# Three 16-head attentions in one kernel: the two halves of each step's scores in a row, the outputs of two steps together, other work behind every second step

## The chip, the core and the metric

The kernel runs on one core of a Trainium2 chip. Its time is the device time of a run in microseconds (us). The core's engines work side by side, each on its own queue in its own order: TensorE (PE, with its weight loads shown apart as PEld), VectorE (DVE), ScalarE (ACT), GpSimd (POOL) and SyncE (SP), which here issues transfers. Semaphores between them hold an instruction until what it reads, or the buffer that it writes, is ready.

## What is computed

The reference is a decoder of two layers on `x` of 4 x 512 tokens, 256 wide. Each layer adds an attention, a cross attention with a context of 1024 tokens, and a feed-forward part to `x`. The change touches three of these, all with 16 heads of 16: the cross attention of the first layer, and the causal attention and the masked cross attention of the second.

```
x = x + L0_attn(layernorm(x));  x = x + L0_xattn(layernorm(x), ctx);  x = x + L0_ffn(layernorm(x))
x = x + L1_attn(layernorm(x));  x = x + L1_xattn(layernorm(x), ctx, mask);  x = x + L1_ffn(layernorm(x))

# L1_xattn; L0_xattn is the same without a mask, L1_attn is causal over the 512 tokens and has a rotation of q and k
query, key_, value = q @ w_q.T + b_q, k @ w_k.T + b_k, v @ w_v.T + b_v         # as [b, 16 heads, s, 16]
scores = einsum('bhqd,bhkd->bhqk', query, key_) / sqrt(16)
scores = where(mask == 0, -1e9, scores)
out = einsum('bhqk,bhkd->bhqd', softmax(scores), value)
return out @ w_o.T + b_o
```

## The kernel before

`heads16` runs these attentions: once for the first layer's cross attention (four parts, one per batch), once for the second layer's two (four causal parts, then four masked ones). A part has four groups `g` of four heads. Each head has 32 partitions of its own, so that four score products can stand on four groups of 32 rows of TensorE at once (`tile_position`). A step is a group and one block of 128 keys: a cross attention has eight steps per group, a causal one four.

The softmax is shifted by each query's largest score, and these maxima are taken ahead of use. So `step(t, u, heads)` does two things at once. For step `t` it makes the transposed scores of four heads (`pa`, L586), whose exponentials ACT writes into `pT` (L605; three buffers). For a step `u` further on it makes plain scores (`pb`, L593), of which DVE takes the row maxima (L626, or L629 where a mask is added). Every product takes a tile of `k.ps()`, a ring of seven PSUM banks (`pools16`); the eighth bank, `av`, gathers outputs. `heads` says which heads of `t` are done; `pb` is shifted by two, so that half a step, two `pa` and two `pb`, fills the four row groups. Products in 32-bit floats are carried out as two passes, and the profile counts each pass.

Where a mask stands, heads 2 and 3 get it by a product of `mask_kT` and a unit matrix on TensorE (L600), heads 0 and 1 by a minimum with `keep_kT` on DVE (L615). In a causal step POOL zeroes the triangle (L609), and the widths shrink: 512, 384, 256 and 128 columns for the four key blocks.

`output` (L661) multiplies `pT` with the values, on four column groups, and adds into `av`; after a group's last block ACT copies `av` to `un` (L669). `lowest` (L638, L641) gathers the maxima of a group, `fold` (L646, L651) transposes them and adds them to the queries three and two steps ahead of the group's first step. `divide` (L676 to L682), `turn` (L693, L698) and `rows` finish a group, a pair and a part. The preparation of the parts to come (norms, projections of queries, keys and values on L125, transfers by `spread`), the making of the masks, and the beginning of what follows are cut into units that `lay` spreads over the slots.

The order is written out by hand for PE, DVE, POOL and SP (`manual_schedule`); ACT's is left to the scheduler. A loop goes over `slots`, each with a step `t`, a step `u`, or both. In every slot with both it issues the first half of the step (heads 0 and 1), then the output of an earlier step (`late` steps back, one in the first run, two in the second), then the second half, then the units in `todo` for this slot.

Of the kernel before, what the change touches and what calls it, by code (L numbers as in the profile page):

```python
# [34 lines left out]
def t_(pool, shape, dtype, tag, bufs=None):  # L35
    return pool.tile(list(shape), dtype, name=tag, tag=tag, bufs=bufs)
# [479 lines left out]
def heads16(k, work, parts, more=(), tail=()):  # L516
# [4 lines left out]

    nc = k.nc
    ng = 4 * len(parts)
    part = lambda g: parts[min(g, ng - 1) // 4]
# [2 lines left out]
    late = 1 if plain else 2  # L529
    start = [0]  # L530
# [3 lines left out]
    total = len(seq)  # L534

    slots, pos, ptr = [], {}, 0
# [10 lines left out]
    def slot(t):  # L547
        return pos[0] + t if t < 0 else pos[t] if t < total else pos[total - 1] + t - total + 1
# [3 lines left out]
    def on_pe(g, h):  # L552
        return part(g).masked is not None and h >= 2

    def step(t, u, heads):


        pa, pb = {}, {}
        if t:
            g, kb = t  # L560
            this = part(g)
            kT, c = batch[g // 4][1], g % 4
            q0 = kb * P if this.causal else 0
            w = S - q0
            if t not in pts:
                pts[t] = t_(work, [P, 4, 512], F32, "pT", 3)
            pT = pts[t]
        if u:
            ug, s = u
            other = part(ug)  # L570
            nh = other.nk // 512
            uqT, ukT = batch[ug // 4][:2]
            uc = ug % 4
            qb, kh = ((1, 0, 3, 2)[s], 0) if other.causal else divmod(s, nh)
            uw = (qb + 1) * P if other.causal else 512
            if ug not in mx:
                mx[ug] = t_(work, [P, TB, nh, 4], F32, f"mx{nh}", 3)
        for h in heads:
            if t:
                pa[h] = k.ps()  # L580
            if u:
                pb[(h + 2) % 4] = k.ps()
        for h in heads:
            if t:
                rows = slice(h * 32, h * 32 + 32)
                nc.tensor.matmul(  # L586
                    pa[h][:, :w], lhsT=kT[rows, c, kb * P : (kb + 1) * P], rhs=q2s[g][rows, q0:],
                    start=True, stop=not on_pe(g, h), tile_position=(h * 32, 0),
                )
            if u:  # L590
                r = (h + 2) % 4
                rows = slice(r * 32, r * 32 + 32)
                nc.tensor.matmul(  # L593
                    pb[r][:, :uw], lhsT=uqT[rows, uc, qb * P : (qb + 1) * P],
                    rhs=ukT[rows, uc, kh * 512 : kh * 512 + uw],
                    start=True, stop=True, tile_position=(r * 32, 0),
                )
        for h in pa:
            if on_pe(g, h):
                nc.tensor.matmul(  # L600
                    pa[h], lhsT=k.identb, rhs=this.masked["mask_kT"][:, kb, :], start=False,
                    stop=True,
                )
        for h in pa:
            nc.scalar.activation(pT[:, h, :w], pa[h][:, :w], AF.Exp)  # L605
        if t and this.causal:

            block = pT[:, heads[0] : heads[-1] + 1, 0:P]
            nc.gpsimd.affine_select(  # L609
                out=block, in_=block, compare_op=ALU.is_ge, fill=0.0, base=0,  # L610
                pattern=[[0, len(heads)], [1, P]], channel_multiplier=-1,
            )
        if t and this.masked and heads[-1] == 3:

            nc.vector.tensor_tensor(  # L615
                pT[:, 0:2], pT[:, 0:2],
                this.masked["keep_kT"][:, kb, :].unsqueeze(1).to_broadcast([P, 2, 512]), ALU.min,
            )
        for r in pb:
            to = mx[ug][:, qb, kh, r : r + 1]  # L620
            if other.causal:
                mask = k.ahead[:, 512 - uw :]
            elif other.masked:
                mask = other.masked["mask_q"][:, qb, kh * 512 : kh * 512 + 512]
            else:
                nc.vector.tensor_reduce(to, pb[r], AX.X, ALU.max)  # L626
                continue
            junk = t_(work, [P, 512], BF16, "junk", 1)
            nc.vector.tensor_tensor_reduce(  # L629
                out=junk[:, :uw], in0=pb[r][:, :uw], in1=mask,  # L630
                scale=1.0, scalar=-3.0e38, op0=ALU.add, op1=ALU.max, accum_out=to,
            )
# [20 lines left out]
    def output(g, kb):  # L653
        v, c = batch[g // 4][2], g % 4
        nkb = size(g)
        q0 = kb * P if part(g).causal else 0
        pT = pts.pop((g, kb))
        if kb == 0:
            avs[g] = t_(k.avp, [P, 512], F32, "av")
        for h in range(4):  # L660
            nc.tensor.matmul(  # L661
                avs[g][h * 32 : h * 32 + 32, q0:],
                lhsT=v[:, kb, (c * 4 + h) * 32 : (c * 4 + h) * 32 + 32],
                rhs=pT[:, h, : S - q0], start=kb == 0, stop=kb == nkb - 1,
                tile_position=(0, h * 32),
            )
        if kb == nkb - 1:
            uns[g] = t_(work, [P, 512], F32, "un", 1)
            nc.scalar.copy(uns[g], avs.pop(g))  # L669
# [30 lines left out]
    def rows(j, i):  # L700
        parts[j].y_rows(i, oTs[j][:, :, i * P : (i + 1) * P])

    todo, load_ = {}, {}

    def at(i, f, *x, pe=0.0):
        todo.setdefault(i, []).append((f, x))
        load_[i] = load_.get(i, 0.0) + pe

    def lay(lo, hi, calls):


        if hi <= 0:
            for f, _ in calls:
                f()
            return
        lo = max(lo, 0)
        there = [load_.get(i, 0.0) + 0.01 for i in range(lo, hi)]
        whole = sum(there) + sum(c for _, c in calls)
        i, sofar = 0, there[0]
        for f, c in calls:  # L720
            while i < hi - lo - 1 and sofar + c / 2 > whole * (i + 1) / (hi - lo):
                i += 1
                sofar += there[i]
            at(lo + i, f, pe=c)
            sofar += c

    marks = []
    for j in range(len(parts)):
        g = start[4 * j]
# [9 lines left out]
    def begin(j):  # L739
        qT, kT, v, chains = parts[j].prep(marks[j])  # L740
        batch[j] = qT, kT, v
        return chains

    ET = mybir.EngineType
    with k.tc.manual_schedule(engines={ET.PE, ET.DVE, ET.Pool, ET.SP}):
        for g in range(ng):
            end = slot(start[g + 1] + late)
            at(slot(start[g] - 3), lowest, g)
            at(slot(start[g] - 2), fold, g, pe=0.45)
            at(end, divide, g, pe=0.45)  # L750
            if g % 2:
                at(end + 1, turn, g, pe=0.45)
            if g % 4 == 3:
                for i in range(TB):
                    at(end + 2 + i // (1 if size(g) > 4 else 2), rows, g // 4, i, pe=0.9)
        for j in range(len(parts)):
            for chain in begin(j):
                lay(*chain)
        for lo, hi, calls in tail:
            lay(len(slots) + lo, len(slots) + hi, calls)  # L760
        for i, u in enumerate(more):
            at(pos[0] + 2 + i * (total - 4 * size(0) - 4) // len(more), u)
        for i in range(len(slots) + late + 6):
            t, u = slots[i] if i < len(slots) else (None, None)
            this = seq[t] if t is not None else None
            ahead = seq[u] if u is not None else None
            both = this and ahead
            if this or ahead:
                step(this, ahead, (0, 1) if both else (0, 1, 2, 3))
            done = t - late if t is not None else i - len(slots) + total - late  # L770
            if (t is not None or i >= len(slots)) and 0 <= done < total:
                output(*seq[done])
            if both:
                step(this, ahead, (2, 3))
            for f, x in todo.pop(i, ()):
                f(*x)


def pools16(k, ctx, name):
# [63 lines left out]
def l0_xattn(k, a):  # L843
    with ExitStack() as ctx:
        wp, work = pools16(k, ctx, "l0x")
        bufs, preset = padded(k, wp, SC)
        k.masked, more = masks(k, work, a)
        parts = cross(k, a, "l0x_", wp, work, bufs, preset)
        heads16(k, work, parts, more=more, tail=ffn_begun(k, a, work))
# [1252 lines left out]
```

## Time and profile before

| what | value |
|---|---|
| median of three runs | 3626.74 us (3625.46 to 3632.22) |
| the profiled execution: time, span | 3623.15 us, 3621.4 us |
| mean granted TensorE clock | 0.966 |
| busy: PE, DVE, ACT, POOL | 94%, 59%, 42%, 27% |
| first cross attention, about | 1031 to 1530 us |
| causal attention, about | 1965 to 2243 us |
| masked cross attention, about | 2243 to 2893 us |

The span is the time from the first to the last instruction of one profiled execution; the run's own time has a little around it. A row of the groups gives line, engine, operation, tiles and count, then the busy time and the mean of one in ns, then the engine's idle time just before them and what ended it. A row of the timeline gives start, length, engine and instruction, with neighbours of one form merged (x2), and in brackets the idle time before it and what released it. PE's instructions overlap, so that the distance from start to start is the time that counts.

### The profile page before, as it was taken

The page shows a single profiled execution, that of the slowest core. Times are in us where ns is not written, and L with a number is a line of the kernel's source. Part 1 is how long each engine was busy: PE and PEld are TensorE (multiplying, and loading weights), DVE is VectorE, ACT ScalarE, POOL GpSimd, SP SyncE. Part 2 cuts the span into 40 slices and gives each one's busy share as a digit, 9 for nine tenths or more (in the row PEclk, how much of TensorE's full clock was granted, in tenths as well). Part 3 has the DMA queues.
Part 4 walks back from the last instruction along what each step waited for, and adds up shares of the span by engine and source line. Part 5 has one row for each costly group of instructions (what it writes and reads, how often), then busy time and mean ns, then how long its engine had stood idle before and what let it go on. Part 6 is the DMA issues. An engine that isn't in the chain of part 4 may idle for free. (4 is left out here: it accounts for less than half of the span.)

```text
span 3621.4 us, 51832 instructions
## 1 busy us (share of the span) xinstructions
PE 3419.2 (94%) x19168; PEld 1593.0 (44%) x19168; DVE 2142.3 (59%) x4804; ACT 1538.0 (42%) x3346; POOL 965.8 (27%) x1185
## 2 busy tenths in 40 slices
PE   7899999997799999999997999999999999999999
PEld 3445454453443333345554444333333344444444
DVE  3575666755477666747785677888888722222211
ACT  2546555465445555554442444445445511111111
POOL 2342433423311021326673322000000022222222
PEclk8899999998899999999997999999999999999999
DMA  3423223241121101000002111010010042111111
GB/s 124 163 82 130 101 96 111 69 152 59 40 41 39 39 27 40 7 21 15 1 1 47 47 44 42 18 24 13 18 28 1 1 156 84 53 47 53 50 52 44
DMA packets 119885, 197.51 MB, mean 55 GB/s; under 512 B 12624, under 2 KB 62800, under 8 KB 117456
## 3 DMA queue, kind: packets, MB, share of 16 engines
q1 hardware_dynamic: 118368, 189.68, 17.2%
q10 hardware_dynamic: 1264, 4.52, 0.4%
q8 instruction: 151, 2.47, 0.3%
q14 instruction: 102, 0.84, 0.1%
HBM read 129.67 MB, written 51.90 MB: 50 GB/s over the span
## 5 line engine op out<-in xcount | busy, mean ns | idle before, releaser
L605 ACT ACTIVATE pT<-ps 128x512 f32<-128x512 f32 (+3 forms) x1280 | 650.9, 565 | 626.4 <-PE ps L593 343.7
L593 PE MATMUL ps<-kT,qT 32*128 32x512 f32 (+3 forms) x2560 | 798.1, 618 | 23.6 <-DMA kT<-way 8.9
L586 PE MATMUL ps<-q,kT 32*128 32x512 f32 (+3 forms) x2560 | 690.6, 609 | 6.8 <-DVE mx L626 6.1
L125 PE MATMUL big<-xnT,w 128*128 128x512 f32 x1024 | 460.3, 592 | 0.0
L1702 DVE TENSOR_TENSOR gu<-big,silu 128x512 f32<-128x512 f32 x136 | 94.1, 692 | 563.5 <-ACT silu L1700 563.5
L626 DVE TENSOR_REDUCE mx<-ps 128x1 f32<-128x512 f32 x512 | 326.5, 685 | 164.2 <-PE ps L593 163.5
L629 DVE CUSTOM_DVE_ANT_0 junk<-ps,mask_q 128x512 bf16<-128x512 f32 x512 | 353.1, 690 | 95.2 <-PE ps L593 27.9
L586 PEld LDWEIGHTS ps<-q,kT 32*128 32x128 f32 x2560 | 214.5, 184 | 349.0 <-ACT pT L605 117.6
L1700 ACT ACTIVATE silu<-big 128x512 f32<-128x512 f32 x136 | 81.2, 597 | 603.8 <-PE big L125 603.8
L1706 POOL TENSOR_TENSOR gu<-gu,cb 128x512 f32<-128x512 f32 x128 | 163.5, 1277 | 633.8 <-DVE gu L1702 503.5
L661 PE MATMUL av<-pT,v 128*32 128x512 f32 (+3 forms) x2560 | 325.3, 578 | 0.5 <-ACT un L669 0.4
L252 POOL TENSOR_TENSOR st<-st,kerm 128x8 f32<-128x8 f32 (+51 forms) x256 | 190.5, 745 | 460.7 <-PE hp L248 398.2
L251 ACT ACTIVATE hd<-hd 128x16 f32<-128x16 f32 (+51 forms) x256 | 162.7, 636 | 344.5 <-DVE hd L250 344.4
L593 PEld LDWEIGHTS ps<-kT,qT 32*128 32x128 f32 x2560 | 259.7, 187 | 103.9 <-DVE mx L629 40.4
L125 PEld LDWEIGHTS big<-xnT,w 128*128 128x128 f32 x1024 | 194.6, 190 | 244.9 <-issue 244.9
L1714 PE MATMUL acc<-gu,w 128*128 128x512 f32 x512 | 241.0, 593 | 1.1 <-POOL gu L1706 1.1
L248 PE MATMUL hp<-st,l0a_w1s 64*128 64x104 f32 (+26 forms) x1024 | 193.4, 456 | 48.6 <-DVE hd L250 48.3
L250 DVE TENSOR_TENSOR hd<-hp,hk 128x16 f32<-128x16 f32 (+51 forms) x256 | 178.5, 697 | 90.8 <-PE hp L248 85.3
L53 POOL TENSOR_TENSOR ln_rstd<-ln_rstd,mhalf 128x4 f32<-128x4 f32 x24 | 24.6, 1023 | 741.6 <-DVE ln_rstd L52 697.1
L260 PE MATMUL ps<-hd,l0a_w 128*64 128x104 f32 (+26 forms) x1024 | 171.4, 414 | 32.3 <-ACT hd L251 26.5
L629 DVE CUSTOM_DVE_ANT_0 junk<-ps,ahead 128x256 bf16<-128x256 f32 (+3 forms) x256 | 125.5, 490 | 75.6 <-PE ps L593 49.2
L1490 ACT ACTIVATE pr<-ps,nmax 128x512 f32<-128x512 f32 x128 | 87.1, 687 | 174.2 <-DVE nmax L1489 173.9
(303 smaller groups left out, 5053.8 us busy)
## 6 DMA issues: line engine op xcount, KB each, us to landing
cb<-comb SPq DMA_DIRECT2D x128, 256.0 KB
scr<-sc SPq DMA_DIRECT2D x108, 256.0 KB
st<-scr SPq DMA_DIRECT2D x16, 1024.0 KB
scr<-sc SPq DMA_DIRECT2D x64, 192.0 KB
st<-scr SPq DMA_DIRECT2D x16, 768.0 KB
w<-in_l1f_w SPq DMA_DIRECT2D x32, 384.0 KB
wqk<-in_l0a_wqk SPq DMA_DIRECT2D x32, 256.0 KB
st<-scr SPq DMA_DIRECT2D x16, 512.0 KB
```

The lines of the kernel that those rows point to most:

```text
L125: k.nc.tensor.matmul(out, lhsT=lhsT(c), rhs=rhs(c), start=start and c == 0, stop=stop and c == 1)
L248: nc.tensor.matmul(hp[:, half, :n], lhsT=w1s[rows], rhs=s[rows, :n], start=True, stop=True)
L250: nc.vector.tensor_tensor(hd[:, :, :n], hp[:, :, :n], hk[:, :, S - n :], ALU.add)
L252: nc.gpsimd.tensor_tensor(s[:, :n], s[:, :n], kerm[:, S - n :], ALU.add)
L260: nc.tensor.matmul(rp[half * 64 : half * 64 + 64, :n], lhsT=w2, rhs=hd[:, half, :n], start=True, stop=True,)
L586: nc.tensor.matmul(pa[h][:, :w], lhsT=kT[rows, c, kb * P : (kb + 1) * P], rhs=q2s[g][rows, q0:], start=True, stop=not on_pe(g, h), tile_po ...
L593: nc.tensor.matmul(pb[r][:, :uw], lhsT=uqT[rows, uc, qb * P : (qb + 1) * P], rhs=ukT[rows, uc, kh * 512 : kh * 512 + uw], start=True, stop ...
L605: nc.scalar.activation(pT[:, h, :w], pa[h][:, :w], AF.Exp)
L626: nc.vector.tensor_reduce(to, pb[r], AX.X, ALU.max)
L629: nc.vector.tensor_tensor_reduce(out=junk[:, :uw], in0=pb[r][:, :uw], in1=mask, scale=1.0, scalar=-3.0e38, op0=ALU.add, op1=ALU.max, accum ...
L661: nc.tensor.matmul(avs[g][h * 32 : h * 32 + 32, q0:], lhsT=v[:, kb, (c * 4 + h) * 32 : (c * 4 + h) * 32 + 32], rhs=pT[:, h, : S - q0], sta ...
L1714: nc.tensor.matmul(accs[b][:, n, :], lhsT=w[e][:, 512 + n * P : 512 + (n + 1) * P], rhs=g, start=e == experts[0], stop=e == experts[-1],)
```

## The change

Only the order in which `heads16` issues its work is changed.

- In every slot with both `t` and `u`, the two halves of the step are issued in a row.
- Outputs come behind every step with an even `t`: those of all steps up to `t - 1` that have not been made, which are two in the steady state. Behind odd steps there are none. After the last slot the rest follow.
- `lowest` and `fold` go into a list of their own, `now`, whose entries run in their slot, behind the outputs. They no longer count in the load that `lay` evens out.
- The other units of a slot (`todo`) run behind odd steps only, those of the even step before and of the odd one together, and behind slots without a `t`.

```diff
-    todo, load_ = {}, {}
+    now, todo, load_ = {}, {}, {}
...
-            at(slot(start[g] - 3), lowest, g)
-            at(slot(start[g] - 2), fold, g, pe=0.45)
+            now.setdefault(slot(start[g] - 3), []).append((lowest, g))
+            now.setdefault(slot(start[g] - 2), []).append((fold, g))
...
+        done = 0
         for i in range(len(slots) + late + 6):
             t, u = slots[i] if i < len(slots) else (None, None)
             this = seq[t] if t is not None else None
             ahead = seq[u] if u is not None else None
-            both = this and ahead
             if this or ahead:
-                step(this, ahead, (0, 1) if both else (0, 1, 2, 3))
-            done = t - late if t is not None else i - len(slots) + total - late
-            if (t is not None or i >= len(slots)) and 0 <= done < total:
+                if this and ahead:
+                    step(this, ahead, (0, 1))
+                    step(this, ahead, (2, 3))
+                else:
+                    step(this, ahead, (0, 1, 2, 3))
+
+
+            last = t - 1 if t is not None and t % 2 == 0 else total - 1 if i >= len(slots) else -1
+            while done <= last:
                 output(*seq[done])
-            if both:
-                step(this, ahead, (2, 3))
-            for f, x in todo.pop(i, ()):
-                f(*x)
+                done += 1
+            for f, x in now.pop(i, ()):
+                f(x)
+            if t is None or t % 2:
+                for j in (i - 1, i):
+                    for f, x in todo.pop(j, ()):
+                        f(*x)
```

## The prediction

> **What bounds the kernel now.** I read the page's busy shares first, then its windows for the three stages that the change touches, then the groups, and last the timeline of TensorE, burst by burst. The three stages are the first cross attention (about 1031 to 1530 us), the causal attention (1965 to 2243) and the masked cross attention (2243 to 2893), some 1430 us of the span.
>
> ```profile
> PE 3419.2 (94%) x19168; PEld 1593.0 (44%) x19168; DVE 2142.3 (59%) x4804; ACT 1538.0 (42%) x3346; POOL 965.8 (27%) x1185
> ...
> L605 ACT ACTIVATE pT<-ps 128x512 f32<-128x512 f32 (+3 forms) x1280 | 650.9, 565 | 626.4 <-PE ps L593 343.7
> L586 PEld LDWEIGHTS ps<-q,kT 32*128 32x128 f32 x2560 | 214.5, 184 | 349.0 <-ACT pT L605 117.6
> ```
> ```profile
> 1200.00:1300.00 100.00, 100.00 (x672) 35.97 (x670) 70.25 (x126) 58.86 (x114) 12.20 (x5) 1.00 0.18 38
> 2460.00:2560.00 100.00, 100.00 (x615) 38.71 (x613) 83.09 (x200) 50.47 (x95) 0.00 (x0) 1.00 0.11 17
> ```
> The columns after the stretch's length are the busy time of PE, PEld, DVE, ACT and POOL, then the granted clock. PE is busy throughout at full clock, DVE at 70% (first stage) and 83% (masked stage), ACT at 50 to 59%. But a busy PE need not be full: the weight loads of the scores (L586) waited 117.6 us for ScalarE's exponentials. So TensorE's order sets the pace, and where PE waits, it waits for a PSUM bank. The timeline of the first stage shows how:
>
> ```profile
> 1295.64 0.69 PE L586 MATMUL ps<-q,kT 32*128 32x512 f32 x1
> 1296.17 0.59 PE L586 MATMUL ps<-q,kT 32*128 32x512 f32 x1
> 1296.71 1.13 PE L125 MATMUL ps<-l0x_wv,cT 128*128 128x256 f32 x4
> 1297.77 0.69 PE L586 MATMUL ps<-q,kT 32*128 32x512 f32 x1
> ...
> 1298.84 1.07 PE L661 MATMUL av<-pT,v 128*32 128x512 f32 x8
> 1299.83 0.69 PE L586 MATMUL ps<-q,kT 32*128 32x512 f32 x1
> ...
> 1300.37 0.59 PE L586 MATMUL ps<-q,kT 32*128 32x512 f32 x1
> ...
> 1300.80 0.60 PE L586 MATMUL ps<-q,kT 32*128 32x512 f32 x2
> ...
> 1300.99 2.06 ACT L605 ACTIVATE pT<-ps 128x512 f32<-128x512 f32 x4 [0.41 <-PE ps L593]
> ...
> 1301.64 0.29 PEld L593 LDWEIGHTS ps<-kT,qT 32*128 32x128 f32 x2 [0.64 <-ACT pT L605]
> 1301.64 1.12 PE L593 MATMUL ps<-kT,qT 32*128 32x512 f32 x2
> ...
> 1302.69 1.06 PE L661 MATMUL av<-pT,v 128*32 128x512 f32 x8
> ```
> Half a step is four score products (two L586, two L593), each in two passes; four stand side by side on the row groups, so half a step is two rounds. Alone it lasts 1.07 us (1295.64 to 1296.71, and 1297.77 to 1298.84). A step's outputs last 1.00 (1298.84 to 1299.83). Where no other work stood between, the second half of one step and the first of the next run in a row, and that lasts 2.86 (1299.83 to 1302.69), not 2.14. The rounds start 0.54, 0.43 and 0.43 apart; the eighth product starts only at 1301.64, when the exponential of the first (from 1300.99) is done. The ring `ps` has seven banks, eight products in a row need eight: the eighth takes the bank of the first. Of such rows 28 stand between two bursts of outputs in the first stage: their median is 2.86, the shortest 2.85, and only three last longer (2.95, 3.68, 3.85).
>
> **The change, part by part.** Counts are from the order of PE's instructions in the two programs, where a burst is a run of one kind.
>
> *1. Both halves of every step in a row.* Every full step is now the pattern that lasts 2.86. The eighth product waits inside its own step, so what stands before the step (outputs, other work) does not relieve it. In narrower steps (causal, width 512, 384, 256, 128) the row costs two halves plus one exponential plus 0.13: 2.14+0.59+0.13=2.86; mixed rows of before fit (a 512 half and a 384 half: 1.07+0.86+0.59+0.13=2.65, and the trace has 2.65; 384 and 256: 2.11, and 2.11). So the price per step is 0.72 at 512, and 0.61, 0.50, 0.40 at the others (exponentials of 0.48, 0.37, 0.27): 0.56 in the mean of the causal stage. Without any wait a row would last 0.54+0.43+0.43+0.53=1.93, a gain of 0.21; that is the lower bound, and 2.86 plus the 0.7 that DVE's lateness costs before in the masked stage is the upper. I take 2.86, as the row of the trace is the same pattern.
> - First stage: rows of eight 31 before, 120 after: 89x0.72=+64. The halves after other work waited already (86 of them, mean 1.18 instead of 1.07, 9 us in all, of which 2 is one long wait): -7.
> - Causal: 57 new rows x0.56=+32; waits there before, 18 us, of which some 8 belong to a stretch at low granted clock around 2040: -10.
> - Masked: 117 new rows x0.72=+84. Here the halves waited most before: after other work 99 with mean 1.63 (55 over 1.07), after the mask's products 22 with mean 2.01 (21 over), 6 elsewhere: 82 us, of which 10 are four long waits that stay: -72.
> By stage +57, +22, +12: together 180 of new waits less 89 of old ones, +91.
>
> *2. Outputs of two steps together.* Two single bursts last 2.00; one burst of four rounds 4x0.43+0.14=1.86. Bursts 127 to 64, 63 to 31, 127 to 65: 157 fewer x0.14=-22 (-9, -4, -9). An output now stands right behind a step's scores, one or two steps after its own exponentials: nothing new is awaited. `pT` has three buffers, and at most three steps are open. The copy `un` then has a step of scores to finish before the next output writes `av`.
>
> *3. Other work behind every second step.* A burst of four L125 passes lasts 1.06, of eight 1.92: joining two saves 0.20. Bursts 96 to 72, 61 to 51, 99 to 69: 64 fewer, -13 (-5, -2, -6). The mask's products (L600) stay 128 bursts; followed by outputs they last 0.54 instead of 0.44, for some 32 more: +3.
>
> *4. What moves with it.* `todo` work of even steps comes up to one step later, with its DVE and ACT evacuations, POOL's powers, bias additions and mask work, and SP's transfers (context, mask, and `spread` of queries and keys: eight issues, 5.2 us on SP). The order of SP's instructions is the same but for one 12.5 KB load two places later; on POOL powers and bias additions move by two to four selects. The last queries of a batch stood on an odd step, two steps before their use, and stay there; the steps grow longer, so the cover of 7.7 us grows. Were it gone, a late transfer would cost at most about 5 us at each of six batch changes; I cost it at nothing. `lowest` and `fold` keep their steps. Behind the eighth product the whole PE queue waits: the outputs or the mask's products, and so DVE and ACT of the next step; DVE needs 2.6 us of maxima per step in the first stage and 4.04 (four maxima and the L615 minimum) in the masked one (2599.62 to 2604.31 in its timeline, less 0.65 of a normalisation), against some 3.9 and 5.1 us per step (500 and 650 us over 128 steps each), so it follows.
>
> Sum: 91-22-13+3=+59 by these terms; by stage +43, +16, 0. I round down to +55, since some of the low-clock waits of the causal stage are swallowed by the new ones. Against the profiled execution: span 3621.4, its time 3623.15, so 3678. The median of the runs shown is 3626.74, 3.6 higher; by that it is 3682. I forecast 3680.
>
> **A rule weighed against the row.** The row: half a step alone takes 1.07, its two rounds at the in-row pace 0.86; so a change of mode costs about 0.2 on this trace. The Trainium skill, "TensorEngine Tiling (Array Packing)", Key Properties, says why: a change of tiling mode, not of tile alone, drains TensorE. It speaks for this change: of 1292 bursts 796 stay. By that rule alone the sum would be 263 joined pairs of halves x0.21=-55, with -22-13+3: -87, so 3540. But the same page, PSUM Bottleneck, says in its own words that tiling "speeds up TensorE but not PSUM evacuation". Rows for that: PE fills a bank every 0.27 us (1.07/4), ACT needs 0.55 to empty one, DVE 0.65. On the mean of a step this is no bound (ACT 2.2, DVE 2.6 of 3.9 us), but within eight in a row it is: the wait takes 0.93, the saved drain gives 0.21. I go by the row of 2.86, which holds both.
>
> **Rivals.**
> - *Faster: the rows don't wait.* The place is the eighth product of each row: if the first one's bank were free when PE reaches it, the sum would be -87, and up to 89 of old waits would go as well: 3540 down to 3451. The turning point: old waits and savings together are -89-22-13+3=-121, so the kernel gets faster once the new waits cost less than 121 of the 180, two thirds of 0.72, which is a row of 2.62 at width 512. For it: after other work or a double burst of outputs ACT is idle when the step begins. Against: in the row shown it was idle too (0.41 us before the exponential at 1300.99), and the ring still has seven banks. 8%.
> - *About the same*: the old waits removed and the savings just meet the new waits, for instance where rows cost 2.62: within 0.2% (about what a measurement of this kernel can tell from no change). 5%.
> - *Much slower: DVE in the masked stage.* If maxima of the step before hold more banks when a row starts, the old waits stay on top: 72+10 us more, about 3750. For it: DVE at 83%. Against: a double burst of outputs (1.86) stands before every second step, and other work before most of the rest. Repeated losses of the granted clock (around 1408 and 2806 it fell to 0.52 for some 6 us after a pause of PE, 3 us each) would look similar on the page; the rows at 1031 to 1052 ran at 1.00, so I expect none. 8%.
> - *As forecast*, +22 to +85: 79%.
>
> **How the numbers follow.** Faster 0.08, same 0.05, slower 0.87. The range: from +22, where the new waits cost four fifths of 180 (144-89-22-13+3=+23), to +85, where a third of the masked stage's old waits stays on top (59+82/3=+86): 3648 to 3712. Beyond it lie faster, same and half of much slower, some 0.18.
>
> **What would show it.** In the timeline of the first stage every step is a run of 16 passes of 2.86, its eighth product with a wait of 0.6 for L605; in the masked one too, with the mask's products behind. The wait of PEld at L586 and L593 for L605 rises from 140 us (117.6+22.6) to over 200. Outputs stand as 16 passes in 1.86. By stage: first +43, causal +16, masked about 0. It is wrong if rows last under 2.6, if the first stage doesn't grow, or if the masked one grows by more than 40.

## The result, and the profile after

The kernel became slower by more than forecast: 3718.2 us (3713.48 to 3723.97) after 3626.1, a ratio of 1.0248 (1.0231 to 1.0264), where 3680 us had been forecast and the range ended at 3712. The sign and the main mechanism were right, the sum was some 38 us short.

From the page after: the row of busy times, and the group of weight loads for the second kind of score, with its busy time and mean, and the idle time before it. These lines of the code stand one lower than before: the scores are L587 and L594, their exponentials L606, the outputs L662.

```profile
PE 3482.2 (94%) x19104; PEld 1699.3 (46%) x19168; DVE 2143.6 (58%) x4804; ACT 1531.9 (41%) x3346; POOL 966.0 (26%) x1185
...
L594 PEld LDWEIGHTS ps<-kT,qT 32*128 32x128 f32 x2560 | 317.9, 189 | 274.3 <-ACT pT L606 136.9
```

DVE, ACT and POOL do the same work in nearly the same busy time. The wait for the exponentials has gone from the first kind of score (L586, 117.6 us before) to the second (L594, 136.9): the waiting product is now mostly the eighth of a row. With 13.1 us at L587 the two waits make 150.0; over 200 had been forecast. The timeline of the first stage, in the same columns as before:

```profile
1203.65 0.69 PE L587 MATMUL ps<-q,kT 32*128 32x512 f32 x1
...
1204.19 0.59 PE L587 MATMUL ps<-q,kT 32*128 32x512 f32 x1
...
1204.62 0.60 PE L587 MATMUL ps<-q,kT 32*128 32x512 f32 x2
...
1204.87 2.06 ACT L606 ACTIVATE pT<-ps 128x512 f32<-128x512 f32 x4 [0.64 <-PE ps L594]
1205.05 0.59 PE L594 MATMUL ps<-kT,qT 32*128 32x512 f32 x1
...
1205.52 1.12 PE L594 MATMUL ps<-kT,qT 32*128 32x512 f32 x2
1206.57 1.92 PE L662 MATMUL av<-pT,v 128*32 128x512 f32 x16
1208.42 0.69 PE L587 MATMUL ps<-q,kT 32*128 32x512 f32 x1
```

A row lasts 2.92 (1203.65 to 1206.57), its eighth product starts at 1205.52, behind the first exponential; two outputs together last 1.85. Both are what the prediction said, to 0.06. The surplus sits elsewhere. This table is summed from PE's timeline, from the start of each burst to the start of the next; S are scores, O outputs, T other work, M the mask's products. The first stage runs from its first transposed score to its last burst of outputs. The masked stage starts with its first mask product and ends with its last burst of outputs; S and M stand together there, as 63 of the 256 records of the mask's products are missing in the trace after. By these records the stages of the kernel before end at 1563.5, 2268.4 and 2890.4 us; the times of the stages given ahead are rough.

| stage | before | after | forecast | change of S, O, T, M |
|---|---|---|---|---|
| first cross attention | 531.8 | 564.0 (+32.2) | +43 | S +50.4, O -9.8, T -8.4 |
| causal | 299.6 | 317.5 (+17.9) | +16 | S +21.3, O -4.9, T +1.5 |
| masked | 622.0 | 666.2 (+44.2) | 0 | S and M +33.3, O -8.5, T +19.3 |

The masked stage grew by more than 40, which the prediction had named as a sign of being wrong. Other work got longer there though its bursts got fewer (99 to 69). Its timeline shows a wait that the kernel before hardly had:

```profile
2597.27 0.60 PE L677 MATMUL ps<-ident,un 128*128 128x128 f32 x4
2597.71 0.68 DVE L630 CUSTOM_DVE_ANT_0 junk<-ps,mask_q 128x512 bf16<-128x512 f32 x1
...
2598.55 0.69 DVE L630 CUSTOM_DVE_ANT_0 junk<-ps,mask_q 128x512 bf16<-128x512 f32 x1
...
2599.16 0.25 DVE L680 RECIPROCAL rec<-ps 128x16 f32<-128x16 f32 x1
2599.45 0.42 DVE L683 TENSOR_TENSOR on<-ps,rec 128x256 f32<-128x256 f32 x1
2599.99 0.54 PEld L694 LDWEIGHTS ps<-ident,on 128*128 128x128 f32 x4 [2.35 <-issue]
2600.02 0.91 PE L694 MATMUL ps<-ident,on 128*128 128x128 f32 x4 [2.15 <-DVE on L683]
```

`divide` transposes a group's outputs on PE (L677), DVE makes `on` from them (L680, L683), and `turn` transposes `on` on PE (L694). Before, a step of scores and outputs stood between `divide` and `turn`. In the second run of `heads16` `late` is two, so `divide` falls on an even slot and `turn` on the odd slot behind it; the change puts the work of both slots into one block. DVE is still at the maxima of the step (L630), and PE waits 2.15 us. The waits at the tile `on`, first of the kernel before, then of the one after (idle us, times):

```profile
L693 PE MATMUL ps<-ident,on x96: 272/273/331, 1109.3 to 2896.0; 128*128 128x128 f32 x96
...
  DVE on L682: 3.7, 4
```
```profile
L694 PE MATMUL ps<-ident,on x96: 272/273/445, 1117.8 to 2989.2; 128*128 128x128 f32 x96
...
  DVE on L683: 40.7, 29
```

These sums take in weight loads and matmuls, and a pause may be counted in both. PE alone waited at `on` for 24.0 us in 17 waits after, for 1.6 in 2 before.

### The profile page after: what moved, and what is told of

Same layout as the page of the kernel before. It is cut to its first block, busy times and chain, and to the rows that moved or that the text cites. A ratio compares the mean times of both kernels' runs of the same rounds, so it can differ in the third digit from the quotient of the medians.

```text
span 3714.7 us, 51779 instructions
## 1 busy us (share of the span) xinstructions
PE 3482.2 (94%) x19104; PEld 1699.3 (46%) x19168; DVE 2143.6 (58%) x4804; ACT 1531.9 (41%) x3346; POOL 966.0 (26%) x1185
## 5 line engine op out<-in xcount | busy, mean ns | idle before, releaser
L594 PE MATMUL ps<-kT,qT 32*128 32x512 f32 (+3 forms) x2560 | 879.2, 612 | 23.0 <-DMA kT<-stage 9.3
L606 ACT ACTIVATE pT<-ps 128x512 f32<-128x512 f32 (+3 forms) x1280 | 639.7, 568 | 616.3 <-PE ps L594 477.1
L587 PE MATMUL ps<-q,kT 32*128 32x512 f32 (+3 forms) x2560 | 665.7, 596 | 2.9 <-ACT pT L606 2.2
L594 PEld LDWEIGHTS ps<-kT,qT 32*128 32x128 f32 x2560 | 317.9, 189 | 274.3 <-ACT pT L606 136.9
L630 DVE CUSTOM_DVE_ANT_0 junk<-ps,mask_q 128x512 bf16<-128x512 f32 x512 | 352.7, 689 | 126.6 <-PE ps L594 86.8
L627 DVE TENSOR_REDUCE mx<-ps 128x1 f32<-128x512 f32 x512 | 319.0, 684 | 158.3 <-PE ps L594 158.3
L587 PEld LDWEIGHTS ps<-q,kT 32*128 32x128 f32 x2560 | 265.8, 187 | 194.3 <-issue 87.3
L662 PE MATMUL av<-pT,v 128*32 128x512 f32 (+3 forms) x2560 | 289.6, 568 | 0.9 <-DVE pT L616 0.9
L630 DVE CUSTOM_DVE_ANT_0 junk<-ps,ahead 128x256 bf16<-128x256 f32 (+3 forms) x256 | 125.5, 490 | 68.6 <-PE ps L594 40.1
L616 DVE TENSOR_TENSOR pT<-pT,held 128x1024 f32<-128x1024 f32 x128 | 156.2, 1220 | 10.1 <-ACT pT L606 10.1
```

Source lines behind the costliest of these rows:

```text
L587: nc.tensor.matmul(pa[h][:, :w], lhsT=kT[rows, c, kb * P : (kb + 1) * P], rhs=q2s[g][rows, q0:], start=True, stop=not on_pe(g, h), tile_po ...
L594: nc.tensor.matmul(pb[r][:, :uw], lhsT=uqT[rows, uc, qb * P : (qb + 1) * P], rhs=ukT[rows, uc, kh * 512 : kh * 512 + uw], start=True, stop ...
L630: nc.vector.tensor_tensor_reduce(out=junk[:, :uw], in0=pb[r][:, :uw], in1=mask, scale=1.0, scalar=-3.0e38, op0=ALU.add, op1=ALU.max, accum ...
L662: nc.tensor.matmul(avs[g][h * 32 : h * 32 + 32, q0:], lhsT=v[:, kb, (c * 4 + h) * 32 : (c * 4 + h) * 32 + 32], rhs=pT[:, h, : S - q0], sta ...
```

## Experiments

The ratios are to the kernel before on the same chip.

**1. `turn` one pair later.** In the kernel after:

```diff
-                at(end + 1, turn, g, pe=0.45)
+                at(end + late, turn, g, pe=0.45)
...
-                    at(end + 2 + i // (1 if size(g) > 4 else 2), rows, g // 4, i, pe=0.9)
+                    at(end + 2 * late + i // (1 if size(g) > 4 else 2), rows, g // 4, i, pe=0.9)
...
-        for i in range(len(slots) + late + 6):
+        for i in range(len(slots) + late + 8):
```

> The changed kernel, but in the second run of heads16 (causal and masked) turn comes one slot later than in it, and so one pair of steps behind divide instead of in the same block of other work; the rows of a part move by two slots with it. Theory A (turn now stands right behind divide and waits on TensorE for VectorE's on, which is queued behind the maxima; 16 times some 2.4 us, with a loss of the granted clock after some of them): the wait of L694 for L683 falls from 41 us to under 8, causal and masked stage lose about 20 us each, the whole comes to 3670 to 3685. Theory B (the surplus of the masked stage is VectorE's lateness in the rows of eight products): the time stays within 10 us of the changed kernel's 3718.

Measured: 3693.1 us, ratio 1.0177 (1.0160 to 1.0193), some 26 us less than the change (1.0248). The first stage is the same to 0.1 us, the causal one loses 11.9, the masked one 15.3, of it 15.2 in T. The wait at `on`:

```profile
L694 PE MATMUL ps<-ident,on x96: 272/273/329, 1120.1 to 2964.3; 128*128 128x128 f32 x96
...
  DVE on L683: 3.8, 4
```

The wait is gone, as theory A said (PE alone waits 1.7 us in 2 waits), but it was worth 26 us, not 40, and the time stayed above theory A's 3670 to 3685; what is left of the masked stage's surplus (28.9) shows that it isn't the whole cause.

**2. The same wait alone, in the kernel before.** `turn` goes into `divide`'s slot in the second run:

```diff
-                at(end + 1, turn, g, pe=0.45)
+                at(end + 2 - late, turn, g, pe=0.45)
```

> The kernel before, with turn put into the same slot as divide in the causal and the masked stage (right behind it), nothing else changed. Theory A: the wait of the changed kernel appears alone: 16 times 2 to 2.6 us, 3655 to 3668, nothing in the first stage. Theory B: turn finds on ready or other work in between, the time stays within 8 us of 3626.

Measured: 3663.3 us, 1.0093 (1.0071 to 1.0115): +34, as theory A expected. The causal stage grows by 22.4 and the masked one by 16.8; the first one, which the edit leaves alone, is the same to 0.1 us. Waits of PE in the whole kernel:

```profile
PE ps L693 <- DVE on L682: 27.7, 17, 3.6
```

The idle time, the number of waits and the longest of them stand in this order. The same row of the kernel before has 1.6 us in 2 waits. So the wait needs nothing of the rest of the change. The granted clock of the causal stage was also lower in this profile (0.91, and 0.94 in the kernel before), which may be why the stages grew by more than the idle time.

**3. The rows alone, in the kernel before.** Both halves in a row, everything else behind every step:

```diff
-            both = this and ahead
             if this or ahead:
-                step(this, ahead, (0, 1) if both else (0, 1, 2, 3))
+                if this and ahead:
+                    step(this, ahead, (0, 1))
+                    step(this, ahead, (2, 3))
+                else:
+                    step(this, ahead, (0, 1, 2, 3))
...
-            if both:
-                step(this, ahead, (2, 3))
```

> The kernel before with the first part of the change alone: both halves of a step in a row; outputs of one step and the other work stand behind every step, at the lags of before. Theory A: rows last 2.86 to 2.92 at width 512 and the wait of turn for divide is absent, so 91 us as the prediction summed for the rows: 3705 to 3725, first stage +50 to +57, causal +15 to +22, masked +12 to +25. Theory B: the masked stage alone grows by 40 or more, the others as in A: 3730 or more.

Measured: 3742.4 us, 1.0313 (1.0298 to 1.0329), +113, in theory B's range of 3730 or more. First stage +53.8, causal +23.4, masked +39.7, with rows of 2.86 at the median in the first stage. So the first two terms of the prediction's rows (+57 and +22) hold within 4 us, and the third (+12) is 28 too small. Scores and mask products of the masked stage together grow by 29.4, its other work by 8.3. This is slower than the whole change. Against experiment 1, which has no wait of `turn` either, it is 49 us slower: summed over the stages, outputs together save 24.8 (22 forecast) and other work together 11.0 (13 forecast). Another 14 lie in scores and mask products, which the prediction did not have; why stays open. Neither of the two joinings was run alone, nor the list `now`.

**4. One product of eight left out.** The kernel after, with the last of the plain scores of each full step left out and its maximum taken a second time from the bank of the product before:

```diff
             if u:
-                pb[(h + 2) % 4] = k.ps()
+                pb[(h + 2) % 4] = pb[0] if t and h == 3 else k.ps()
...
-            if u:
+            if u and not (t and h == 3):
                 r = (h + 2) % 4
```

> The changed kernel with one of the eight products of a full step left out (the last of the plain scores, for head 1 of the group ahead); its maximum is taken from the bank of head 0 instead, so VectorE and ScalarE do as many instructions as before. A row then needs seven banks. The four row groups' rounds are as many as before, so that TensorE's own time doesn't fall. Theory A (the eighth product waits for the first one's bank): rows fall from 2.9 to about 2.0 at width 512, the wait of the score weight loads for L606 nearly goes, first stage -100 or so, the masked stage less (VectorE has 4.5 of 5.2 us per step), all in all 3500 to 3570. Rival C (a row is long because ScalarE and VectorE can't empty four banks each any faster, or for the order of row groups): rows stay over 2.6 and the time within 40 us of 3718.

Measured: 3594.8 us, 0.9905 (0.9890 to 0.9921), 123 us under the kernel after. The first stage falls by 75.0 to 489.0, the causal one by 15.8, the masked one by 33.3. The row in the first stage:

```profile
1201.10 0.69 PE L587 MATMUL ps<-q,kT 32*128 32x512 f32 x1
...
1201.63 0.59 PE L587 MATMUL ps<-q,kT 32*128 32x512 f32 x1
...
1202.07 0.60 PE L587 MATMUL ps<-q,kT 32*128 32x512 f32 x2
...
1202.26 2.07 ACT L606 ACTIVATE pT<-ps 128x512 f32<-128x512 f32 x4 [0.58 <-PE ps L594]
...
1202.50 0.60 PE L587 MATMUL ps<-q,kT 32*128 32x512 f32 x2
1203.03 1.92 PE L662 MATMUL av<-pT,v 128*32 128x512 f32 x16
```

1.93 us (1201.10 to 1203.03) instead of 2.92, the value worked out before for a row without a wait, though the four rounds are still there and ACT and DVE do as many instructions. ACT is at its four exponentials until 1204.33, long after the row's end, and nobody waits for them. So the row's length was the eighth bank, and rival C falls. The time stays above theory A's 3500 to 3570: rows in the masked stage, taken at their weight loads, last 2.24 at the median, but 34 of 117 exceed 3.0. PE waits there for DVE's maxima at the scores for 26.4 us, and `turn` still waits (21.6).

**5. Both: seven products, and `turn` one pair later.**

> Both at once: one of the eight products of a full step left out as before (the maximum of head 1 of the group ahead is taken from head 0's bank), and turn one slot later in the causal and the masked stage. Theory A: the wait for the bank and the wait for divide are two different things and add: 3594.8 less 25, 3563 to 3577. Rival: with seven products TensorE is no longer the bound where turn waits, and it brings under 8 us: 3587 or more.

Measured: 3567.0 us, 0.9825 (0.9797 to 0.9852). It adds up as theory A says, and is faster than both kernels. The softmax doesn't depend on the shift, but a head shifted by another's maximum has lost its guard against overflow; so this is a measurement of the order, not a replacement.

**6. Seven products in the kernel before.** The same edit of `step`, with the order of before.

> The kernel before with the same one product of eight left out (the last of the plain scores in each full step; its maximum taken from head 0's bank), in the order of before. If the bank of the eighth product is what rows cost, the 31 rows of the first stage fall from 2.86 to 1.93 (-29), those of the causal stage by some 4, and the old waits of the masked stage by a part of 72: 3550 to 3590. Compared with f1 it tells what the changed order is worth where its rows don't wait: by the prediction's terms (drains saved 55 in the halves, 22 in outputs, 13 in other work) f1 should then be faster than this one by 30 or more; if not, the old order wasn't paying these drains on the path.

Measured: 3590.2 us, 0.9881 (0.9862 to 0.9900), at the upper end. The rows of the first stage fall to 1.92 at the median, though the stage loses 15.7 where 29 was expected. Half a step with three products lasts 1.06 there, one with four 1.07: leaving a product out shortens nothing by itself.

Against it experiment 5 is 23 us faster, less than the 30 that was to show drains on the path. By the profiles the gain lies in the first stage alone (25.8); the causal stage is 5.2 slower and the masked one 7.8. The profile of experiment 5 is of its slowest run (3581.66, the others 3562.33 to 3571.02), so that the last two may be too high. Of the 25.8, 18.7 lie in the outputs, which last 7.0 longer in experiment 6 than in the kernel before, and 9.0 in the scores, where 89 joined pairs at 0.21 make 19. So where the bank is there, the changed order is the better one in the first stage; how much of that is drains stays open. In the masked stage DVE stands in the way: PE waits 31.9 us for its maxima at the scores in experiment 5, 12.2 in experiment 6.

**7. The masked stage without the minimum.** Experiment 1, with the mask of heads 0 and 1 left out:

```diff
-        if t and this.masked and heads[-1] == 3:
+        if False and heads[-1] == 3:
```

> The kernel with turn later (first experiment), with the minimum that masks heads 0 and 1 in the masked stage left out: VectorE has 1.2 us less per step there, 128 times, and nothing else changes on TensorE. Theory D (what is left of the masked stage's surplus, rows over 3.0 us and the waits of score loads for L630, is VectorE's lateness): scores and mask products of that stage fall by 12 to 25 us, the whole to 3668 to 3681. Rival (these are losses of the granted clock and the row's own 2.92): within 6 us of 3693.

Measured: 3674.3 us, 1.0117 (1.0097 to 1.0137), some 22 us under experiment 1. The masked stage in the windows, experiment 1 and then this one (after the length: busy PE, PEld, DVE, ACT and POOL, the granted clock, the DMA share and GB/s):

```profile
2308.00:2959.00 651.00, 633.99 (x3678) 268.43 (x3740) 515.26 (x1242) 315.68 (x601) 13.08 (x16) 0.99 0.07 13
```
```profile
2299.00:2932.00 633.00, 620.82 (x3677) 255.68 (x3740) 386.28 (x1128) 313.13 (x600) 13.09 (x16) 1.00 0.07 14
```

DVE's busy time falls by 129 us, and the stage by 17.7 (650.9 to 633.2), 13.7 of it in scores and mask products, though no instruction of TensorE changed. By the weight loads, rows over 3.0 us fall from 15 to 4, the mean row from 3.03 to 2.93. The clock differs by 0.01 of 650, so up to 6 of the 17.7 may be the granted clock. The rest is DVE's lateness: theory D. The four longest rows of experiment 1 (4.48 to 5.85 by the weight loads) show how it comes about. The second of them:

```profile
2490.41 0.73 DVE L83 TENSOR_SCALAR ln_xn<-x,ln_mv,ln_rstd 128x256 f32<-128x256 f32 x2 [1.13 <-POOL ln_rstd L53]
...
2492.51 1.22 DVE L616 TENSOR_TENSOR pT<-pT,held 128x1024 f32<-128x1024 f32 x1
...
2494.39 1.12 PE L594 MATMUL ps<-kT,qT 32*128 32x512 f32 x2 [0.63 <-DVE mx L630]
```

A normalisation waits for POOL at the head of DVE's queue, the step's maxima and the minimum (L616) come late behind it, and the row waits for a bank that DVE still holds. The same stands before the other three. No run leaves the minimum out of the kernel before, so what it costs there isn't known.

## Why the prediction was wrong

- **The rows** were right in kind, place and price in the first two stages (+57, +22): experiment 4 takes the eighth bank's need away and rows fall to the 1.93 that was worked out. In the first stage the scores grew by 50.4 where 57 was summed; in the causal one by 21.3 for 22, of which 3.5 go with the wait of `turn` (17.8 in experiment 1). A row lasts 2.92 in most places where 2.86 was taken: in the first stage 2.92 behind two outputs (35 of 38), 2.86 behind four passes of other work (22 of 23). What makes these 0.06 stays open.
- **Outputs together** (-9, -4, -9) measured -9.8, -4.9 and -8.5. **Other work together** (-5) measured -8.4 in the first stage.
- **The step that failed first: "What moves with it", costed at nothing.** The part looked at transfers, at `lowest` and `fold`, and at the distance of outputs from their exponentials. It didn't look at what stands inside a block that now holds two slots' work: `divide` and `turn` depend on each other through DVE. That is 26 us by experiment 1, and 34 alone in experiment 2. The causal stage's forecast of +16 met the measured +17.9 by luck: without this wait (11.9) it grows by some 6, as scores cost less and other work saves more than was summed.
- **The term that was mis-sized: the masked stage, forecast at 0.** The prediction took 72 of 82 us of old waits as replaced by the wait inside the row. The rows alone (experiment 3) cost +39.7 there. Experiment 7 shows a part of why: with DVE relieved, rows come to 2.93 and the stage loses 17.7, of which up to 6 may be the clock. DVE "follows" on the mean of a step, as was said, but not in each. The prediction's 4.04 us for DVE left a normalisation of 0.65 out, and its 5.1 us per step are 4.86 (622.0 over 128 steps); the longest rows of experiment 1 stand just behind normalisations. This was the third rival, "DVE in the masked stage", at about a fifth of its price (17.7 of 82). With the minimum left out 11.2 remain over the kernel before (633.2 to 622.0): 4.6 over the forecast in scores and mask products, and 6 in other work, which saves nothing there where 6 was forecast. Their cause stays open.
- By stage against the forecast: the first one 11 less; the causal one 10 less, and 11.9 more for `turn`; the masked one 44.2 more, of it 15.3 for `turn`, at most 17.7 for DVE, 11.2 open.
- **The rule weighed against the row** was rightly held below it here; by the rule alone the kernel would have come to 3540. What the joined halves save was there too: rows without the bank's wait last 1.93, two halves 2.14. But with the wait away the changed order gains 23 us over the old one, all in the first stage, and not the 87 of the rule's sum. What decided was the bank.

## What to carry to other kernels

Before joining bursts to save their change of mode, count the banks that one burst needs and compare with the ring: one bank too few cost 0.93 to 0.99 us per row here, more than four times the 0.21 that joining saved. When work of two slots is put into one block, look for pairs in it that depend on each other through another engine: the distance between them was cover. And beside an engine as busy as DVE in the masked stage (83%), a part of the waits counted "replaced" by a new wait stayed on top of it: look at the steps in which that engine has the most to do, and not at the mean step.

## What was not expected of the hardware

After a pause of PE of 2.15 us (2597.87 to 2600.02) the granted clock was 0.54 for the next 2.5 us in the kernel after; after one of 2.35 (2683.72 to 2686.07) it stayed at 1.00. The windows of these stretches, in the same columns:

```profile
2600.00:2602.50 2.50, 2.48 (x8) 1.74 (x8) 0.00 (x0) 0.58 (x1) 0.00 (x0) 0.54 0.00 0
```
```profile
2687.00:2691.00 4.00, 3.84 (x27) 1.47 (x30) 2.56 (x6) 2.60 (x7) 0.00 (x0) 1.00 0.02 4
```

By an estimate from the first of these windows (0.46 of 2.50 us) such a wait cost some 1.2 us more by the clock, but not each time; the sums above count it where it fell.
